# Norm statistics by sums on ScalarE, and attention weights of four steps added by accumulating DMAs

## The chip, the cores and the metric

The kernel runs on one core of a Trainium2 chip. The metric is the device time of one execution in microseconds (us). A run is one execution; medians are over several runs of the same kernel.

Engines, as the profile names them: PE is TensorE's matmuls, PEld its weight loads, DVE VectorE, ACT ScalarE, POOL GpSimd, SP SyncE. SPq and POOLq are the queues on which SP and GpSimd issue DMAs.

## The reference, cut to what matters

Sixteen graphs ("batches") of 1024 nodes with 256 features go through four layers. Each layer normalises its input; three are graph attention, the fourth is a small transformer block of eight heads of 32 features.

```python
def _layernorm(x, axis=-1, eps=1e-5):
    m = jnp.mean(x, axis=axis, keepdims=True)
    v = jnp.var(x, axis=axis, keepdims=True)
    return (x - m) / jnp.sqrt(v + eps)
...
# layers 0 to 2: h = relu(layernorm(x)); x = x + graph_attention(h, adj, W, a)
# layer 3, on h = relu(layernorm(x)), with H = 8 heads of D = 32:
scores = jnp.einsum('fnhd,fmhd->fhnm', q, k) / sqrt(D)
scores = jnp.where(mask, scores, -1e9)
attn = softmax(scores, axis=-1)
t = jnp.einsum('fhnm,fmhd->fnhd', attn, v).reshape(F, N, C)
x = _layernorm(x + t, ln1_g, ln1_b)
h = relu(x @ w1 + b1)
x = _layernorm(x + h @ w2 + b2, ln2_g, ln2_b)
```

Two things matter here: the means and variances of the norms, and the denominators of layer 3's softmax, which are sums of the exponentials over all 1024 keys.

## The kernel before

The kernel contains its own planner. Every operation is recorded with an engine, an estimated duration and the buffers that it reads and writes; `schedule` then plays the engines against each other and fixes the order of each engine at build time. Priorities come from a few numbers, the "constants" (`GATS`, `VALUES`, `STEPS`, `FEED`, `LEAD`, `BIAS`).

Layer 3 walks through `steps` of (group of four heads `g`, half of the rows `hf`, block of 128 keys `jt`). A step makes the scores of four heads, takes the exponential on ScalarE and multiplies by the mask on VectorE, into two tiles `pa` of 128 x 1024 fp32 (512 KB each). A "quad" of matmuls on 32 columns each then multiplies them with the values, and another quad with a tile of ones gives the denominators. In three of the four groups of a batch, the weights of two steps were first added on VectorE, so that one ones quad served two steps:

```python
                if paired(g, hf) and jt % 2:
                    sums[n] = [r_sums.new() for _ in range(2)]
                    for ss, p0, p1 in zip(sums[n], pas[n - 1], pas[n]):
                        dve(tt_us(2 * HALF), lambda: nc.vector.tensor_add(ss.t, p0.t, p1.t), [ss], [p0, p1])
```

The projections for the scores are split into a high and a low part and copied into stacks `qs` and `ks` by 16 small DMAs from SP. `hi` and `lo` are single buffers, and a projection shares its four PSUM buffers `sc` with the scores.

```python
            pe(CT * mm_us(HALF), product, [sc], ...)          # sc: one of 4 PSUM buffers
            act(act_us(HALF), lambda: nc.scalar.copy(hi.t.bitcast(F32R), sc.t), [hi], [sc])
            dve(tt_us(HALF), lambda: nc.vector.tensor_sub(lo.t, sc.t, hi.t), [lo], [sc, hi])
            for a in range(4):
                part = ((hi, hi, lo, lo), (hi, lo, hi, lo))[keys][a]
                for r in range(HG):
                    dma(0.33, lambda: nc.sync.dma_start(
                            stack.t[a * D3 : (a + 1) * D3, r, at : at + HALF],
                            part.t[r * D3 : (r + 1) * D3, :]), ..., us=0.635)
        ...
        later = {
            (0, 0, 2): [(queries, 0, 1)],
            (0, 1, 2): [(queries, 1, 0)],     # issued during group (0, 1)
            (0, 1, 4): [(keys, 1, 0)],
            (1, 0, 0): [(keys, 1, 1)],
            (1, 0, 2): [(queries, 1, 1)],
        }
```

Norm statistics were made on VectorE, 256 features at a time:

```python
    def stats(src, src_ref, dst, dst_ref, whose="g"):
        st = r_st[whose].new()
        dve(0.342, lambda: nc.vector.bn_stats(st.t, src), [st], [src_ref])
        dve(0.11, lambda: nc.vector.bn_aggr(dst, st.t), [dst_ref], [st])
```

Of the kernel before, what the change touches and what calls it, by code (L numbers as in the profile page):

```python
# [16 lines left out]
AF = mybir.ActivationFunctionType  # L17
# [242 lines left out]
LANDING = 2.5  # L260
BIAS = 0.648
LEAD = {"act": -0.527, "dve": 0.112}
# [38 lines left out]
def direct(ctx, tc, flag, x, adj, gat_w, gat_a, w_qkv, ln1_g, ln1_b, ln2_g, ln2_b, w1, b1, w2, b2, out):  # L301
# [12 lines left out]
        (-0.447, -0.367, -0.162, 0.113, 0.24),  # L314
        (0.384, 0.522, 0.626, 0.731, 0.828),
        (0.805, 0.841, 0.856, 0.879, 1.02),
    )
    VALUES = (1.045, 1.057, 1.088, 1.245, 1.191)
    STEPS = (1.289, 1.484, 1.664, 1.807, 1.951)
    FEED = (2.178, 2.28, 2.353, 2.529, 2.38)  # L320
# [37 lines left out]
    r_st = {k: ring(f"st{k}", 4, [6]) for k in "gf"}  # L358
    r_hn = ring("hn", 1, [TH, C])
# [46 lines left out]
    def dve(us, emit, w, r):  # L406
        rec.add("dve", us, emit, w, r)
# [7 lines left out]
    def stats(src, src_ref, dst, dst_ref, whose="g"):  # L415
        st = r_st[whose].new()
        dve(0.342, lambda: nc.vector.bn_stats(st.t, src), [st], [src_ref])  # L417
        dve(0.11, lambda: nc.vector.bn_aggr(dst, st.t), [dst_ref], [st])

# [213 lines left out]
    def gat(xt, b_mv, b_rstd, l):  # L633
# [8 lines left out]
        for hf in range(2):  # L642
# [3 lines left out]
            inverse(mv[:, l, s, 0], mv[:, l, s, 1], rstd[:, l, s], mv_refs, rstd_ref)  # L646
# [142 lines left out]
        for hf in range(2):  # L789
            s = slice(hf * TH, (hf + 1) * TH)  # L790
            if H == 1:
                row = spread(hf, 0, rds[hf])
                pts = [weights(hf, 0, jt, row) for jt in range(NT)]
                for k in range(TH):
# [55 lines left out]
                    dve(tt_us(C), lambda: nc.vector.tensor_add(xs, xs, ex), [xt(it)], [b_ex(0)])  # L850
                    if l != 1:
                        dve(
                            tt_us(C),
                            lambda: nc.vector.tensor_sub(xs, xs, eo),
                            [xt(it)],
                            [b_ex(1)],
                        )
                    stats(xs, xt(it), mv[:, l + 1, it, :], b_mv((l + 1, it)))
# [116 lines left out]
    def attention(b, xt, b_mv, b_rstd):  # L975
# [3 lines left out]
        for hf in range(2):  # L979
# [3 lines left out]
            inverse(mv[:, 3, s, 0], mv[:, 3, s, 1], rstd[:, 3, s], mv_refs, rstd_ref)  # L983
# [122 lines left out]
        def quad(ac, jt, of_head, columns, first, last):  # L1106
            for r in range(HG):
                nc.tensor.matmul(  # L1108
                    ac.t[r * D3 : (r + 1) * D3, :],
                    columns(r),  # L1110
                    of_head(r),
                    start=first,
                    stop=last,
                )

        def value(n, both):

            g, hf, jt = steps[n]
            for ac in accs[g, hf][: 1 + both]:
                quad(  # L1120
                    ac,
                    jt,
                    lambda r: pas[n][r // 2].t[:, r % 2, :],
                    lambda r: (
                        ones
                        if ac is accs[g, hf][1]
                        else va.t[:, jt, (g * HG + r) * D3 : (g * HG + r + 1) * D3]
                    ),
                    jt == 0,
                    jt == NT - 1,  # L1130
                )

        def paired(g, hf):

            return g == 1 or hf == 1
# [4 lines left out]
        for n in range(len(steps) + LAG):  # L1140
            m = n - LAG
            if m >= 0:
                g, hf, jt = steps[m]
                if jt == 0:
                    accs[g, hf] = [r_bank.new(), r_bank.new()]
                both = not paired(g, hf)
                pe(
                    (1 + both) * 0.855,
                    lambda: value(m, both),
                    accs[g, hf],  # L1150
# [3 lines left out]
                if not both and jt % 2:  # L1154
                    ss = sums[m]
                    pe(
                        0.855,
                        lambda: quad(
                            accs[g, hf][1],
                            jt,  # L1160
                            lambda r: ss[r // 2].t[:, r % 2, :],
                            lambda r: ones,
                            jt == 1,
                            jt == NT - 1,
                        ),
                        [accs[g, hf][1]],
                        ss,
                        ("col4", "col4"),
                    )
# [51 lines left out]
            if n < len(steps):  # L1221
# [56 lines left out]
                if paired(g, hf) and jt % 2:  # L1278
                    sums[n] = [r_sums.new() for _ in range(2)]
                    for ss, p0, p1 in zip(sums[n], pas[n - 1], pas[n]):  # L1280
                        dve(
                            tt_us(2 * HALF),
                            lambda: nc.vector.tensor_add(ss.t, p0.t, p1.t),  # L1283
                            [ss],
                            [p0, p1],
                        )
# [3 lines left out]
    def feed(b, x3, hn):  # L1290
# [95 lines left out]
        def back(hf):  # L1386
            yT = yTs[hf]
            for it in (hf * TH, hf * TH + 2):
# [32 lines left out]
                act(act_us(HALF), lambda: nc.scalar.copy(z_t, pz()), [z(0), z(1)], [g])  # L1421
                for k in range(2):
                    stats(z_t[:, k, :], z(k), mvz.t[:, k, :], mvz(k), "f")
                inverse(
                    mvz.t[:, :, 0], mvz.t[:, :, 1], rstdz.t, [mvz(0), mvz(1)], rstdz, False
                )
                for k in range(2):
# [8 lines left out]
                            op0=ALU.subtract,  # L1436
# [29 lines left out]
    def batch(b):  # L1466
# [12 lines left out]
        for it in range(NT):  # L1479
            stats(xt.at(it), xt(it), b_mv.t[:, 0, it, :], b_mv((0, it)))  # L1480
# [630 lines left out]
```

## Time and profile before

| kernel before | |
|---|---|
| time | 4209.74 us, median of 3 runs (4208.88 to 4213.89) |
| PE, DVE, ACT, POOL busy | 98, 88, 55, 10% of the span |
| TensorE idle | 33 us in the first 200, 20 in the last 109, 18.5 from 200 to 3800 |

The page's chain of work that ended last, as shares of the span by engine:

```profile
PE 80%; DVE 12%; DMA 2%; SPq 2%; issue 2%; POOL 1%; ACT 1%; DVEq 0%; ACTq 0%
```

Two rows of waits (engine, tile and line that waited, what ended the wait, us in total, times, longest):

```profile
DVE pt L774 <- DMA row<-rd: 78.6, 30, 7.3
...
ACT pa L1259 <- DVE sums L1283: 54.8, 28, 2.7
```

### The profile page before, as it was taken

Reading aid. Unit: us, or ns where it says so; the run is one execution under the profiler, and the core shown is the slowest. Engines: PE = TensorE matmul, PEld = TensorE weight load, DVE = VectorE, ACT = ScalarE, POOL = GpSimd, SP = SyncE. Lnnn points to the kernel's source line nnn. Section 1 sums busy time; section 2 is a strip of 40 time slices with the busy share of each in tenths; the row PEclk is TensorE's granted clock in tenths of the full one; section 3 lists DMA queues with packets and bytes.
Section 4 is the critical chain, followed back from the end, with each engine's and each line's share of the span. In section 5 each row is a group of like instructions: output and inputs, shape, how many; then the busy total and the mean of one; then the engine's idle time right before and its main releaser. Section 6 shows DMA issues by size and latency. Waiting matters only on the chain.

```text
span 4208.8 us, 68595 instructions
## 1 busy us (share of the span) xinstructions
PE 4133.7 (98%) x24738; PEld 2399.0 (57%) x24738; DVE 3710.0 (88%) x6786; ACT 2333.7 (55%) x5041; POOL 427.2 (10%) x391
## 2 busy tenths in 40 slices
PE   7999999999999999999999999999999999999998
PEld 3746556564665646556465564646656465564643
DVE  7589898998989889898998979989898898989977
ACT  3445555564655746556555555646556465565564
POOL 0001001011010101001010010110111010010110
PEclk9999999999999999999999999999999999999998
DMA  3121222212222122221212222122221222212131
GB/s 104 48 64 42 81 61 66 66 36 81 58 74 61 51 65 57 76 71 52 66 45 81 61 66 66 36 81 59 73 60 50 65 58 76 69 49 67 44 86 36
DMA packets 180683, 263.82 MB, mean 63 GB/s; under 512 B 41328, under 2 KB 76400, under 8 KB 180336
## 3 DMA queue, kind: packets, MB, share of 16 engines
q1 hardware_dynamic: 180336, 259.36, 22.5%
q8 instruction: 198, 3.24, 0.3%
q14 instruction: 149, 1.22, 0.1%
HBM read 91.03 MB, written 33.95 MB: 30 GB/s over the span
## 4 chain that ended last, share of the span: by engine, by line
PE 80%; DVE 12%; DMA 2%; SPq 2%; issue 2%; POOL 1%; ACT 1%; DVEq 0%; ACTq 0%
PE bank L801 21%; PE bank L1108 16%; PE sc L1235 10%; PE bank L677 8%; DVE pt L774 7%; PE bank L875 6%; PE bank L474 5%; PE sc L1024 5%; PE bank L1341 4%; PE bank L885 3%; DVE pa L1268 2%; PE sc L1060 2%; SPq L1045 2%; DMA row<-rd 1%; POOL rstdz L426 1%
## 5 line engine op out<-in xcount | busy, mean ns | idle before, releaser
L1259 ACT ACTIVATE pa<-sc 128x512 f32<-128x512 f32 x2048 | 1096.4, 607 | 588.4 <-PE sc L1235 448.6
L1268 DVE TENSOR_TENSOR pa<-pa,mask 128x1024 f32<-128x1024 f32 x1024 | 1210.1, 1211 | 12.4 <-ACT pa L1259 12.0
L774 DVE SCALAR_TENSOR_TENSOR pt<-row,e,mask 128x512 f32<-128x512 f32 x1536 | 1058.5, 740 | 107.5 <-DMA row<-rd 78.6
L801 PE MATMUL bank<-qb,pt 128*128 128x257 f32 x4096 | 942.8, 381 | 0.5 <-ACT ex L829 0.4
L801 PEld LDWEIGHTS bank<-qb,pt 128*128 128x128 f32 x4096 | 770.6, 190 | 166.5 <-issue 21.8
L1235 PE MATMUL sc<-qs,ks 128*128 128x512 f32 x2048 | 700.4, 448 | 1.9 <-ACT pa L1259 1.3
L1108 PE MATMUL bank<-pa,va 128*32 128x512 f32 x4096 | 543.5, 597 | 7.4 <-DVE pa L1268 7.0
L875 PE MATMUL bank<-pt,qb 128*32 128x512 f32 x4096 | 511.5, 596 | 4.7 <-DVE pt L774 4.7
L1235 PEld LDWEIGHTS sc<-qs,ks 128*128 128x128 f32 x2048 | 358.0, 188 | 223.7 <-ACT pa L1259 102.7
L1283 DVE TENSOR_TENSOR sums<-pa,pa 128x1024 f32<-128x1024 f32 x384 | 454.6, 1213 | 7.0 <-PE bank L1108 6.5
L677 PE MATMUL bank<-w_aug,hT 128*128 128x259 f32 (+1 forms) x1536 | 372.8, 391 | 0.6 <-ACT mask L587 0.2
L426 POOL TENSOR_TENSOR rstd<-rstd,neg_half 128x4 f32<-128x4 f32 x160 | 200.7, 1257 | 1499.8 <-DVE rstd L423 1340.9
L677 PEld LDWEIGHTS bank<-w_aug,hT 128*128 128x128 f32 x1536 | 289.4, 192 | 94.4 <-issue 15.3
L875 PEld LDWEIGHTS bank<-pt,qb 128*32 128x32 f32 x4096 | 132.8, 109 | 303.4 <-issue 210.3
L829 ACT ACTIVATE ex<-bank,rec 128x256 f32<-128x256 f32 x256 | 121.6, 476 | 324.0 <-DVE rec L821 321.1
L885 PE MATMUL bank<-pt,e 128*32 128x512 f32 x2048 | 288.4, 593 | 0.0
L1108 PEld LDWEIGHTS bank<-pa,va 128*32 128x32 f32 x4096 | 118.8, 109 | 283.1 <-issue 196.5
L445 ACT ACTIVATE hn<-xt,mv,rstd 128x256 f32<-128x256 f32 x384 | 204.2, 598 | 87.7 <-DVE mv L435 87.7
L906 ACT COPY ot<-bank 128x512 f32<-128x512 f32 x128 | 75.0, 586 | 318.7 <-PE bank L875 269.7
L1024 PE MATMUL sc<-hTa,wqkv_sb 128*128 128x512 f32 x512 | 239.9, 595 | 1.0 <-ACT hTa L1009 0.5
L1108 PE MATMUL bank<-sums,ones 128*32 128x512 f32 x1536 | 216.4, 597 | 0.7
L417 DVE BATCH_NORM_STATS2 stg<-xt 128x6 f32<-128x256 f32 x512 | 208.9, 414 | 3.2
(107 smaller groups left out, 4053.0 us busy)
## 6 DMA issues: line engine op xcount, KB each, us to landing
row<-rd SPq DMA_DIRECT2D x192, 256.0 KB
ks<-hi SPq DMA_DIRECT2D x512, 64.0 KB
ks<-lo SPq DMA_DIRECT2D x512, 64.0 KB
qs<-hi SPq DMA_DIRECT2D x512, 64.0 KB
qs<-lo SPq DMA_DIRECT2D x512, 64.0 KB
xt<-in_x_dram SPq DMA_DIRECT2D x32, 512.0 KB
x<-xt SPq DMA_DIRECT2D x32, 512.0 KB
xr<-x SPq DMA_DIRECT2D x64, 256.0 KB
```

What stands on the lines that cost most here:

```text
L426: lambda: nc.gpsimd.tensor_tensor(out=rstd, in0=rstd, in1=neg_half[:, :n], op=ALU.pow),
L677: nc.tensor.matmul(g.t[:, : C + 3 * H], hT.t[:, ct, k * P : (k + 1) * P], w_aug[l][:, ct, :], start=ct == 0, stop=ct == CT - 1,)
L774: lambda: nc.vector.scalar_tensor_tensor(pt.t, row.t, e3[:, 2, jt // TH, h, jt % TH : jt % TH + 1], mask[:, jt, hf * HALF : (hf + 1) * HAL ...
L801: nc.tensor.matmul(g.t[:, : D + 1], pts[jt].t[:, k * P : (k + 1) * P], qb[:, jt, 0, :], start=jt == 0, stop=jt == NT - 1,)
L875: nc.tensor.matmul(g.t[u * D + d : u * D + d + D3, :], qb[:, j, h + u, d : d + D3], pts[u][j - jt].t, start=j == 0, stop=j == NT - 1,)
L885: nc.tensor.matmul(gd.t[c : c + D3, :], one(jt + k, h + u).to_broadcast([P, D3]), pts[u][k].t, start=jt == 0, stop=jt == NT - 2,)
L1024: nc.tensor.matmul(sc.t, wqkv_sb[:, ct, c0 : c0 + P], hT.t[:, ct, hf * HALF : (hf + 1) * HALF], start=ct == 0, stop=ct == CT - 1,)
L1108: nc.tensor.matmul(ac.t[r * D3 : (r + 1) * D3, :], columns(r), of_head(r), start=first, stop=last,)
L1235: nc.tensor.matmul(scs[r - r0].t, ks.t[:, r, jt * P : (jt + 1) * P].bitcast(F32R), q.t[:, r, :].bitcast(F32R), start=True, stop=True,)
L1259: lambda: nc.scalar.activation(pt.t[:, v, :], sc.t, AF.Exp, scale=1.0 / math.sqrt(D3)),
L1268: lambda: nc.vector.tensor_mul(pt.t, pt.t, mask[:, jt : jt + 1, i0 : i0 + HALF].to_broadcast([P, 2, HALF]),),
L1283: lambda: nc.vector.tensor_add(ss.t, p0.t, p1.t),
```

## The change

The intent is to take work from TensorE (fewer ones quads) and from VectorE (statistics), and to give it to ScalarE and to the DMA engines, which have room. Means come as a by-product of the last add on VectorE or of a copy on ScalarE, and variances as a sum of squares on ScalarE. The weights of four steps are added in the groups with `hf == 1`, the third and the fourth step by a DMA that adds to its target; the other groups add two steps; the last batch adds none.

```diff
-LANDING = 2.5
-BIAS = 0.648
-LEAD = {"act": -0.527, "dve": 0.112}
+LANDING = 2.8
+BIAS = 0.939
+LEAD = {"act": 2.715, "dve": 0.501}
 ... (GATS, VALUES, STEPS, FEED: other numbers too)
+    def spread_of(srcs, src_refs, sums, squares, refs):
+        act(0.19, lambda: nc.scalar.mul(sums, sums, -1.0 / C), refs, [])
+        for k, (src, src_ref, ref) in enumerate(zip(srcs, src_refs, refs)):
+            act(act_us(C, 1) + 60e-3,
+                lambda: nc.scalar.activation(waste.t, src, AF.Square,
+                    bias=sums[:, k : k + 1], accum_out=squares[:, k : k + 1]), [ref], [src_ref])
 ... (the end of a graph layer)
-                    dve(tt_us(C), lambda: nc.vector.tensor_add(xs, xs, ex), [xt(it)], [b_ex(0)])
-                    ...
-                    stats(xs, xt(it), mv[:, l + 1, it, :], b_mv((l + 1, it)))
+                    dve(stt_us(C) + 60e-3,
+                        lambda: nc.vector.scalar_tensor_tensor(
+                            xs, xs, 0.0, last, op0=ALU.add, op1=op, accum_out=total), ...)
 ... (layer 3)
-        def paired(g, hf):
-            return g == 1 or hf == 1
+        def run_of(g, hf):
+            return 1 if b == NB - 1 else 4 if hf == 1 else 2
 ...
+                run = run_of(g, hf)
+                if jt % run == 1:
+                    sums[g, hf] = [r_sums.new() for _ in range(2)]
+                    ... (ss = p0 + p1 on VectorE, as before)
+                elif jt % run:
+                    for ss, pt in zip(sums[g, hf], pas[m]):
+                        dma(3.0, lambda: nc.gpsimd.dma_start(ss.t, pt.t, accum_op=ALU.add),
+                            [ss], [pt], us=0.88, engine="pool")
 ... (the value quad)
+                if jt % run == run - 1:
+                    ss = pas[m] if run == 1 else sums[g, hf]
+                    ... (one ones quad for the run)
```

The second norm of the feed-forward and the first norm of each batch change in the same way; the statistics of the first feed-forward norm and those of one graph layer stay as they were.

## The prediction

> **What bounds the kernel now.** I read the busy table first, then the same numbers by stretches of time, then the order of TensorE's matmuls, and the groups that the change touches last.
>
> ```profile
> PE 4133.7 (98%) x24738; PEld 2399.0 (57%) x24738; DVE 3710.0 (88%) x6786; ACT 2333.7 (55%) x5041; POOL 427.2 (10%) x391
> ...
> PE   7999999999999999999999999999999999999998
> ```
>
> TensorE is at 98%, VectorE at 88%, ScalarE at 55%, GpSimd at 10%. A busy TensorE need not be a full one, so I asked where it is not busy, by stretches (columns: stretch, its length, then busy time and instructions of PE, PEld, DVE, ACT, POOL, then clock, DMA share, GB/s):
>
> ```profile
> 0.00:100.00 100.00, 76.94 (x528) 34.08 (x530) 81.10 (x176) 28.62 (x57) 4.48 (x12) 0.95 0.32 109
> 100.00:200.00 100.00, 89.96 (x392) 70.84 (x387) 53.28 (x153) 43.44 (x108) 9.52 (x14) 0.93 0.11 36
> ...
> 2000.00:2600.00 600.00, 595.99 (x3722) 335.02 (x3712) 542.80 (x986) 332.99 (x715) 61.25 (x54) 1.00 0.22 62
> ...
> 4100.00:4209.00 109.00, 89.28 (x386) 33.65 (x384) 85.00 (x134) 50.78 (x94) 5.60 (x7) 0.90 0.14 36
> ```
>
> Of the 75 us in which TensorE is idle (4208.8 - 4133.7), 33 lie in the first 200 us and 20 in the last 109. In the middle it is idle for 4 us of 600. There VectorE with 543 of 600 is not what TensorE waits for; the program fixes the order ahead of time, and other batches fill the gaps. So in the middle the time is the sum of what TensorE is given, and work taken from VectorE alone buys next to nothing.
>
> The timeline of TensorE's matmuls (start, duration, line, tiles, count) says what one unit of that work is worth. Durations overlap, so I go by start to start:
>
> ```profile
> 1016.50 1.92 PE L875 MATMUL bank<-pt,qb 128*32 128x512 f32 x16
> 1018.24 1.04 PE L885 MATMUL bank<-pt,e 128*32 128x512 f32 x8
> 1019.10 1.90 PE L875 MATMUL bank<-pt,qb 128*32 128x512 f32 x16
> 1020.81 1.04 PE L885 MATMUL bank<-pt,e 128*32 128x512 f32 x8
> 1021.79 1.20 PE L1235 MATMUL sc<-qs,ks 128*128 128x512 f32 x4
> 1022.91 1.92 PE L875 MATMUL bank<-pt,qb 128*32 128x512 f32 x16
> ```
>
> Eight records on 32 columns each (four fp32 matmuls of two passes, a "quad" below) take 0.86 us in a stream (1018.24 to 1019.10). Four score matmuls between other 128-column work take 0.92 us (0.23 each, from the trace's starts). From 1016.50 to 1022.91 there are six quads and four scores, 6 x 0.858 + 0.92 = 6.07, but 6.41 passed: leaving the 32-column work and coming back to it costs 0.34 us. Over the whole trace the return trips without an evident wait give a median of 0.34 to 0.36 us. I count 352 such blocks in the kernel before.
>
> **What the Trainium skill says.** "Perfetto Trace Analysis", section "Identifying the Most-Contended Engine": matmul busy time is not a good measure of distance from the roofline, because matmuls are pipelined. I agree for this trace, where the quad's records read 1.04 us for a step of 0.86, and therefore use steps. "TensorEngine Tiling (Array Packing)", section "Key Properties": changing the tiling mode drains TensorE; the 0.34 us above is this trace's number for it. "DMA: Bandwidth & Descriptors", section "Anatomy of one DMA": a DMA issued by GpSimd takes about 2.0 us plus bytes / 436e3; a section further on (SWDGE vs HWDGE vs iDMA) says that accumulating needs this path. The kernel before has none, so no run here shows it yet. "ScalarE: Activation LUTs", section "What ACT_TABLE_LOAD costs": 186 ns + 0.833 per element with immediates, 93 more per pointer operand, so 399 and 492 ns for 256 elements; the trace has 425 (the second Relu of the ELU) and 476 (the scaled Relu), within 7%. For the accumulator output the page has no price.
>
> **The change, part by part.** The groups that it touches:
>
> ```profile
> L1283 DVE TENSOR_TENSOR sums<-pa,pa 128x1024 f32<-128x1024 f32 x384 | 454.6, 1213 | 7.0 <-PE bank L1108 6.5
> ...
> L1108 PE MATMUL bank<-sums,ones 128*32 128x512 f32 x1536 | 216.4, 597 | 0.7
> L417 DVE BATCH_NORM_STATS2 stg<-xt 128x6 f32<-128x256 f32 x512 | 208.9, 414 | 3.2
> ...
> L1108 PE MATMUL bank<-pa,ones 128*32 128x512 f32 x1024 | 149.5, 593 | 0.0
> ```
>
> *Denominators on TensorE.* Before, each batch spends 8 quads with the ones in its first group and 4 in each of the other three: 20, times 16 batches = 320 (the counts agree: (1536 + 1024) / 8). After, batches 0 to 14 spend 4 + 2 + 4 + 2 = 12, and the last batch sums nothing and spends 32: 180 + 32 = 212. So 108 quads go, at 0.858 us = -92.7 us. But the order of the built kernel has 430 32-column blocks instead of 352: the sums' quads now often stand between scores instead of next to a value quad. 78 x 0.34 = +26.5 us. Net on the bounding engine: **-66 us**.
>
> *Sums on VectorE.* 24 adds per batch stay (16 for the pairs of two groups, 8 for the first pairs of the runs of four), and 24 of the last batch go: -24 x 1.18 = -28 us.
>
> *Statistics on VectorE.* 384 of the 512 statistics of xt and the 128 of the second norm of the feed-forward go, each with its aggregation: 512 x about 0.56 (busy time by group) = -287 us. In return 256 plain adds become adds with a total, some 0.06 to 0.12 dearer: +15 to +30. With the sums VectorE falls from 3710 to about 3420 us. By the stretches above this is off the path except at the ends.
>
> *ScalarE.* Per batch 16 copies with a total (0.43), less 4 wide copies (0.62), 32 squares with a pointer (0.48) and 10 small scalings (0.2): about 22 us, or +345 us, to some 2680 us, 65%. Off the path, but the way through a norm gets longer: four squares can only follow all four totals, about 2 us later than an aggregation did.
>
> *DMA and GpSimd.* 15 batches x 2 groups x 2 runs x 2 steps x 2 tiles = 240 transfers of 512 KB. By the skill's formula, an estimate, 2.0 + 1.2 = 3.2 us each; reading the target as well makes it nearer 4.5. They run two and two, and the fourth step's must wait until the third's have landed. In the order of the built kernel, the work that lies on TensorE between the last score of a run of four and the quad that reads its sum is at least 13.2 us (by the steps above), in the median 16. What must fit: an exponential 0.6, a mask product 1.2, two issues of perhaps 1 us each, two transfers of 2.5 us one behind the other and a landing of 2, some 11 us. So mostly hidden, with little room in about 15 of the 60 cases.
>
> *The ends.* The last batch runs without a next one beside it. There VectorE has 2.4 + 1.2 us per step (two mask products, and one add on average) against about 2.6 of TensorE. Without sums it has 2.4 and TensorE 3.1; of 20 us idle I expect some 10 to 15 to go (the 12 quads more are counted above). The first 200 us are a single batch's chain, and the longer norms may cost about 5 there.
>
> Sum: 4210 - 66 - 12 + 5 = 4137. VectorE's lower load should take away some of the short waits of the middle (20 us idle, and by the steps some 57 us above the plain sum), and I give it 10 us, less a few for late sums: **4130 us**.
>
> **The rivals.** *Late sums.* If an accumulating transfer takes 6 us instead of 3 to 4, or the descriptors take GpSimd several us, TensorE, whose order is fixed, stands at some of the 60 sums quads for 2 to 6 us, and 1/sqrt of the norms stands behind the transfers in GpSimd's queue: +60 to +200 us, so 4190 to 4330. For it: no such transfer in the trace; against: 13 to 16 us of cover. *Contention of transfers.* The DMA share is 22% now, and 240 x 512 KB add at least 126 MB to 259. The rows' broadcasts already make VectorE wait (78.6 us in 30 waits) and could be held up by a few us each: +10 to +40 us. *VectorE was the hidden bound*, through buffers that it frees late: then taking 8% of its work gives more than the sum, 4080 to 4100. Against it are the 4 us of 600. *Switching dearer than counted*, with most of the gain lost in the drains: 4150 to 4170.
>
> **Range and chances.** The quads (-93) are certain, the switches are uncertain by 10, the bubbles by 25 and the sums by more on the slow side. 8 in 10: 4095 to 4172. Faster by over 2% means under about 4127, which is almost the middle: 0.44. Within 2%: 0.52. Slower by over 2%: 0.04.
>
> **What would show it.** TensorE still at 98 to 99% and its records down by 864 to 23874; 848 ones matmuls in program terms (1696 records); VectorE near 3420, ScalarE near 2680. Sums in time: waits of TensorE on a landing of the accumulating transfer below 15 us in all. Wrong if those waits exceed 60 us, if GpSimd's 1/sqrt is late and the norms stop TensorE, or if TensorE's idle time in the middle stretches falls or rises by more than 10 us in 600.

## More of the kernel before

A transfer is planned like this, with a queue for each issuing engine of its own:

```python
            if x.moved:
                queue[e] = max(at + 0.2, queue[e]) + x.moved
                x.pass_on = queue[e] + LANDING - (at + us)
```

VectorE carries 12% of the chain though TensorE is hardly ever idle: the chain goes through VectorE at times. Its longest wait for a transfer is for the rows that are broadcast for the graph attention.

## The result, and the profile after

| | median of 4 runs | range |
|---|---|---|
| before | 4211.11 us | 4208.88 to 4213.89 |
| after | 4155.49 us | 4152.05 to 4163.23 |
| ratio | 0.9870 | 0.9853 to 0.9887 (95%) |

A ratio is the mean time of one kernel's fast runs over that of the other's of the same rounds, so it is not quite the ratio of the medians quoted. The change is worth 1.3%: within 2%, inside the range, and 25 us above the predicted 4130.

The busy table of the kernel after, and from the same page its chain by engine, its two large DMA queues (packets, MB, share of 16 engines' span) and the row of its accumulating transfers (count, KB each, median us from issue to landing):

```profile
PE 4049.7 (98%) x23874; PEld 2358.5 (57%) x23874; DVE 3504.5 (84%) x5994; ACT 2680.9 (65%) x6673; POOL 558.7 (13%) x631
...
q1 hardware_dynamic: 180336, 259.36, 22.3%
q0 software_dynamic: 34560, 125.84, 16.0%
...
PE 79%; ACT 8%; DVE 6%; DMA 2%; SPq 2%; issue 2%; POOL 0%; DVEq 0%; ACTq 0%
...
sums<-pa POOLq DMA_DIRECT2D x240, 512.0 KB, 5.9
```

TensorE is busy as large a share as before. Half of VectorE's share of the chain has gone, and ScalarE has taken as much. A queue that did not exist before uses 16.0% of the DMA engines: 0.160 x 4150.3 / 240 = 2.8 us of all sixteen for each transfer.

The stretches of the kernel after (columns as in the prediction):

```profile
0.00:100.00 100.00, 77.92 (x535) 34.77 (x536) 78.46 (x162) 42.22 (x110) 6.14 (x13) 0.97 0.32 109
100.00:200.00 100.00, 88.81 (x386) 72.12 (x384) 42.48 (x119) 52.02 (x153) 6.89 (x12) 0.90 0.09 29
...
2000.00:2600.00 600.00, 592.54 (x3548) 344.29 (x3541) 531.23 (x900) 393.90 (x986) 85.93 (x93) 1.00 0.40 96
...
4050.00:4151.00 101.00, 83.21 (x487) 34.16 (x486) 65.25 (x102) 58.57 (x132) 5.80 (x7) 0.95 0.17 44
```

The ends have hardly moved: 33.3 us of TensorE idle in the first 200 (33.1 before), 17.8 in the last 101 (19.7 in the last 109 before). The middle has become worse: 7.5 us idle of 600 where it was 4.0, and 40.7 from 200 to 3800 where it was 18.5.

The groups that the change touched, by form (columns as in the prediction):

```profile
L1188 DVE TENSOR_TENSOR sums<-pa,pa 128x1024 f32<-128x1024 f32 x360 | 435.6, 1221 | 30.3 <-PE bank L1161 25.3
...
L1161 PE MATMUL bank<-sums,ones 128*32 128x512 f32 x1440 | 193.5, 599 | 0.2 <-DMA sums<-pa 0.2
...
L418 DVE BATCH_NORM_STATS2 stg<-xt 128x6 f32<-128x256 f32 x128 | 49.3, 416 | 0.0
...
L1161 PE MATMUL bank<-pa,ones 128*32 128x512 f32 x256 | 37.6, 593 | 0.0
```

The ones quads fell from 2560 records to 1696, as counted. They idle 0.2 us for a landing of the sums, so the sums are in time.

**The time taken apart.** Busy time hides short stands between matmuls, so I took TensorE's matmul records of each trace and worked with their starts. Each kind of matmul has a median step from its start to the next start (for example 0.2175 us for the 257 columns of the graph layers, 0.4293 for 512 columns, 0.230 for scores, 0.1073 for a record of a quad). Count times step is the *plain sum*. Blocks of 32-column work times 0.345 us are the *switches*. What is left between the first and the last matmul's start is the *rest*: all waiting and all slowness. I give the rest of the stretch from 250 to 3890 us apart.

| us | plain sum | switches (blocks) | rest | of it 250 to 3890 |
|---|---|---|---|---|
| before | 3920 | 121 (352) | 144 | 54 |
| after | 3827 | 148 (430) | 153 | 80 |
| difference | -93 | +27 | +9 | +26 |

The three differences make -57, and the profiled spans differ by -58.5 (4208.8 and 4150.3). So the two certain terms of the prediction came out as worked, and the rest, which should have shrunk by some 14 us (ends -7, middle -10 and a few for late sums), grew by 9.

Where does the middle lose? The waits have two rows which answer to those of before, and two new ones:

```profile
ACT pa L1319 <- DVE sums L1188: 68.3, 36, 5.0
...
DVE pt L813 <- DMA row<-rd: 35.8, 24, 7.3
PE sc L1295 <- DVE lo L1089: 35.7, 14, 4.2
...
PEld bank L1161 <- DMA sums<-pa: 2.8, 4, 1.1
```

TensorE stood 14 times before scores, 2.5 us on average, until VectorE had made a low part `lo`. Before, PE had no such wait for the scores of attention steps (line 1235 of that kernel). Fourteen is close to one for each of the fifteen batches that add by DMA. The rows' broadcasts, which I had feared for, wait less than before, and the sums quads wait for landings for 2.8 us in the whole kernel.

One of the fourteen, in stretches of 5 us around it (columns as before: the last three are clock, DMA share and GB/s), and then its timeline (start, duration, engine and line, operation, tiles; in brackets the idle time before it and what ended that):

```profile
2825.00:2830.00 5.00, 5.00 (x24) 4.03 (x22) 5.00 (x9) 2.54 (x5) 0.40 (x1) 1.00 0.57 110
2830.00:2835.00 5.00, 5.00 (x31) 1.91 (x31) 4.43 (x7) 2.59 (x6) 1.38 (x2) 1.00 1.04 234
2835.00:2840.00 5.00, 2.19 (x10) 1.53 (x9) 1.54 (x5) 2.01 (x4) 1.56 (x2) 1.00 1.06 218
2840.00:2845.00 5.00, 4.93 (x15) 3.97 (x16) 4.59 (x8) 2.25 (x5) 0.17 (x1) 0.66 0.99 211
```

```profile
2827.88 7.89 SPq L1098 DMA_DIRECT2D qs<-lo  x8
...
2829.60 0.92 POOL L1196 DMA_DIRECT2D sums<-pa  x1 [9.63 <-DVE sums L1188]
...
2832.77 1.98 PE L1077 MATMUL sc<-hTa,wqkv_sb 128*128 128x512 f32 x4
...
2835.87 4.89 SPq L1098 DMA_DIRECT2D ks<-hi  x4
...
2836.61 0.58 PE L1295 MATMUL sc<-qs,ks 128*128 128x512 f32 x1
...
2839.32 0.69 DVE L1089 TENSOR_TENSOR lo<-sc,hi 128x512 f32<-128x512 f32 x1 [3.46 <-DMA qs<-lo]
...
2840.07 1.43 PE L1295 MATMUL sc<-qs,ks 128*128 128x512 f32 x3 [2.87 <-DVE lo L1089]
```

Read it from the top. SP issues the eight copies of the low part of the queries of group (1, 0), which takes 7.89 us. Among them GpSimd issues accumulating transfers, and the DMA engines are full: a share of 1.04, then 1.06, at 234 and 218 GB/s (the share adds up the times of packets, which must overlap where it passes 1). Meanwhile TensorE has made the projection of the keys (2832.77). Its low part must go into the one buffer `lo`, which the copies of the queries still read, so VectorE, whose order is fixed, stands 3.46 us. The projection's PSUM buffer is one of the four that the scores use, and the scores stand 2.87 us until VectorE has read it.

The stand costs more than its own length. In the last of the four stretches the granted clock is 0.66: its record reads 0.5 from 2840.3 to 2843.8 us, and there the matmuls of 257 columns go at steps of 0.43 us in place of 0.2175. Between 250 and 3890 us this trace has eight stretches at 0.5, of 3.4 or 6.8 us, and each begins 2.8 to 4.5 us after the last matmul start before one of these stands. The eight stands were 2.9 to 4.7 us long; two others of 3.5 and 3.8 us and all shorter ones were not followed by such a stretch. By steps, the matmuls in the eight stretches lost some 16 us. The kernel before has no such stretch there, and no two of its matmul starts there lie more than 1.3 us apart.

### The profile page after: what moved, and what is told of

Read it like the earlier page. It is cut to its first block, busy times and chain, and to the rows that moved or that the text cites. A ratio compares the mean times of both kernels' runs of the same rounds, so it can differ in the third digit from the quotient of the medians.

```text
span 4150.3 us, 68028 instructions
## 1 busy us (share of the span) xinstructions
PE 4049.7 (98%) x23874; PEld 2358.5 (57%) x23874; DVE 3504.5 (84%) x5994; ACT 2680.9 (65%) x6673; POOL 558.7 (13%) x631
## 3 DMA queue, kind: packets, MB, share of 16 engines
q1 hardware_dynamic: 180336, 259.36, 22.3%
q0 software_dynamic: 34560, 125.84, 16.0%
## 4 chain that ended last, share of the span: by engine, by line
PE 79%; ACT 8%; DVE 6%; DMA 2%; SPq 2%; issue 2%; POOL 0%; DVEq 0%; ACTq 0%
PE bank L840 18%; PE bank L1161 12%; PE sc L1295 10%; PE bank L927 10%; PE bank L716 7%; PE bank L512 5%; PE bank L937 5%; PE bank L1392 5%; PE sc L1077 4%; ACT waste L429 2%; PE sc L1113 2%; SPq L1098 2%; DVE pa L1328 2%; ACT pa L1319 1%; DVE pt L813 1%
## 5 line engine op out<-in xcount | busy, mean ns | idle before, releaser
L1319 ACT ACTIVATE pa<-sc 128x512 f32<-128x512 f32 x2048 | 1108.1, 607 | 448.7 <-PE sc L1295 317.5
L813 DVE SCALAR_TENSOR_TENSOR pt<-row,e,mask 128x512 f32<-128x512 f32 x1536 | 1068.1, 747 | 49.6 <-DMA row<-rd 35.8
L1161 PE MATMUL bank<-pa,va 128*32 128x512 f32 x4096 | 514.7, 597 | 1.3 <-DVE pa L1328 1.0
L1188 DVE TENSOR_TENSOR sums<-pa,pa 128x1024 f32<-128x1024 f32 x360 | 435.6, 1221 | 30.3 <-PE bank L1161 25.3
L716 PE MATMUL bank<-w_aug,hT 128*128 128x259 f32 (+1 forms) x1536 | 391.2, 393 | 2.1 <-ACT hT L710 1.9
L1196 POOL DMA_DIRECT2D sums<-pa x240 | 210.5, 877 | 1059.4 <-DVE rec L860 239.0
L927 PEld LDWEIGHTS bank<-pt,qb 128*32 128x32 f32 x4096 | 122.3, 109 | 296.5 <-issue 224.0
L429 ACT ACTIVATE waste<-xt,mv 128x256 f32<-128x256 f32 x384 | 196.2, 511 | 7.0
L1161 PE MATMUL bank<-sums,ones 128*32 128x512 f32 x1440 | 193.5, 599 | 0.2 <-DMA sums<-pa 0.2
L1086 ACT CAST hi<-sc 128x512 fp32r<-128x512 f32 x128 | 74.5, 582 | 178.9 <-PE sc L1077 76.9
```

The costliest lines, as they stand in the source:

```text
L429: lambda: nc.scalar.activation(waste.t, src, AF.Square, bias=sums[:, k : k + 1], accum_out=squares[:, k : k + 1]),
L716: nc.tensor.matmul(g.t[:, : C + 3 * H], hT.t[:, ct, k * P : (k + 1) * P], w_aug[l][:, ct, :], start=ct == 0, stop=ct == CT - 1,)
L813: lambda: nc.vector.scalar_tensor_tensor(pt.t, row.t, e3[:, 2, jt // TH, h, jt % TH : jt % TH + 1], mask[:, jt, hf * HALF : (hf + 1) * HAL ...
L927: nc.tensor.matmul(g.t[u * D + d : u * D + d + D3, :], qb[:, j, h + u, d : d + D3], pts[u][j - jt].t, start=j == 0, stop=j == NT - 1,)
L1161: nc.tensor.matmul(ac.t[r * D3 : (r + 1) * D3, :], columns(r), of_head(r), start=first, stop=last,)
L1319: lambda: nc.scalar.activation(pt.t[:, v, :], sc.t, AF.Exp, scale=1.0 / math.sqrt(D3)),
```

## The experiments

Four theories for the missing 25 us, the first two of which are rivals for the same stands:

- **Contention.** The bytes of the accumulating transfers fill the DMA engines just when SP's stack copies need them. The cure is fewer bytes at that moment.
- **The order.** The new order itself puts the copies and the scores too close, or the many small issues do; the transfers' bytes don't matter.
- **VectorE matters.** I had called its load off the path. If it is on it after all, the statistics gave more than counted and hid a larger loss.
- **Late sums**, which the 2.8 us above already speak against.

All expectations below are from before the runs. Where they number the theories, 1 is contention and 2 the order; their theory 3 is that GpSimd's queue, with the transfers in it, makes the 1/sqrt of the norms late. Where only the accumulating line is replaced, the planner sees the same record as before, so each engine keeps its order.

| kernel | median us | ratio to before (95%) | gaps over 1 us within scores: number, us | rest | of it 250 to 3890 |
|---|---|---|---|---|---|
| after | 4155.5 | 0.9870 (0.9853 to 0.9887) | 15, 45.2 | 153 | 80 |
| none_added (wrong) | 4101.1 | 0.9743 (0.9726 to 0.9759) | 1, 1.3 | 99 | 28 |
| half_bytes (wrong) | 4107.3 | 0.9755 (0.9739 to 0.9771) | 7, 10.4 | 108 | 36 |
| two_halves | 4155.9 | 0.9866 (0.9850 to 0.9883) | 14, 38.1 | 156 | 82 |
| gpsimd_adds | 4524.6 | 1.0749 (1.0731 to 1.0767) | 30, 119.6 | 525 | 393 |
| one_by_dve | 4152.8 | 0.9862 (0.9846 to 0.9879) | 6, 10.5 | 150 | 76 |
| both_by_dve | 4271.0 | 1.0141 (1.0124 to 1.0158) | 16, 41.3 | 273 | 182 |
| stats_alone | 4243.1 | 1.0080 (1.0063 to 1.0097) | 2, 2.6 | 138 | 39 |
| stats_alone_replanned | 4179.4 | 0.9927 (0.9912 to 0.9943) | 2, 3.0 | 91 | 3 |
| sums_alone_old | 4419.6 | 1.0487 (1.0470 to 1.0505) | 2, 6.4 | 426 | 342 |
| sums_alone_replanned | 4264.3 | 1.0126 (1.0111 to 1.0142) | 14, 52.2 | 264 | 182 |
| one_queue | 4136.7 | 0.9827 (0.9812 to 0.9842) | 2, 3.5 | 129 | 51 |
| one_queue_q_early | 4131.1 | 0.9815 (0.9801 to 0.9828) | 0, 0 | 126 | 54 |

The kernel before has no such gap. The plain sum is 3920 for the two kernels with the statistics alone and 3827 for the others but before. All results were correct except for the two that are wrong on purpose. Matmuls at half clock are part of the rest: between 250 and 3890 us they lost some 16 us in after, 11 in two_halves, 88 in gpsimd_adds, 34 in both_by_dve, 43 in sums_alone_old and 23 in sums_alone_replanned. The other kernels, the kernel before among them, have no half-clock stretch there.

### Without the transfers

```diff
-                            lambda: nc.gpsimd.dma_start(ss.t, pt.t, accum_op=ALU.add),
+                            lambda: None,
```

The third and fourth steps are missing from the sums, so the result is wrong (relative error 0.07).

> The 240 accumulating transfers are left out, everything else keeps its place in every engine's order (the result is wrong on purpose: the third and fourth step are missing in the sums). Theory 1 (the transfers hold the DMA engines while the copies of q and k into their stacks run, so the first scores of a group come late once per batch, 49 us in all by the start times of the matmuls): the once-per-batch gap of 2.9 to 4.7 us at the scores goes below 1 us and the time is 4105 to 4120 us. Theory 2 (the fixed order puts that projection of q too late, whatever the transfers do): the gap stays at 3 to 4 us and the time at 4145 to 4160. Theory 3 (GpSimd's queue makes the 1/sqrt late): the gap at the scores stays, other idle time of TensorE in the middle falls, 4130 to 4150.

Measured: 4101.13 us, 54 less than after. The gaps within scores go from 15 (45.2 us) to 1 (1.3 us), and the rest of the middle from 80 to 28. Of these 52 us, 39 are steps of over 1 us between matmul starts (less the matmuls' own) and 16 the half clock; other terms give 3 back. The same copies in SP's queue in this trace:

```profile
2798.84 4.94 SPq L1098 DMA_DIRECT2D qs<-lo  x8
...
2806.02 2.41 SPq L1098 DMA_DIRECT2D ks<-hi  x4
```

They take 4.94 and 2.41 us where they took 7.89 and 4.89, in the same order of instructions. Over the whole trace, 14 of 48 such groups of eight took more than 6 us with the transfers, and 1 of 48 without. So the transfers cost 54 us, which makes the order theory fall for them, and without them the middle is better than before the change (28 against 54). What this run can't tell is whether it is their bytes, their number or GpSimd's issue of them.

### Half of each transfer

```diff
-                            lambda: nc.gpsimd.dma_start(ss.t, pt.t, accum_op=ALU.add),
+                            lambda: nc.gpsimd.dma_start(ss.t[:, 0, :], pt.t[:, 0, :], accum_op=ALU.add),
```

Wrong as well: the same 240 transfers, of 256 KB each.

> Same order, same 240 accumulating transfers, but each moves half of its columns (wrong result on purpose). Theory 1: the gap at the scores shrinks to about 1 to 2.5 us, time 4120 to 4140, between no transfers and whole ones. Theory 2: as the changed kernel, 4145 to 4160. Theory 3: as the changed kernel too, since GpSimd issues as many transfers.

Measured: 4107.34 us, below the expected 4120 to 4140, so 48 of the 54 us go with half of the bytes. The number of issues is the same, and GpSimd is as busy (562.0 us against 558.7). The landing falls from 5.9 to 3.6 us in the median, SP's eight copies take 5.69 us, and the stands before scores nearly vanish; in the waits:

```profile
PE sc L1295 <- DVE lo L1089: 5.8, 7, 1.2
```

Neither the number of transfers nor their issue matters then, but the bytes do, and far from in proportion: half of them cost 6 us, all of them 54. The half clock is one reason that the traces show: with half of the bytes no two matmul starts in the middle lie more than 1.9 us apart and no stretch at half clock follows. That the DMA engines are full at that moment or not would be another; it is argued and not shown apart.

### The same bytes in twice as many transfers

```diff
-                            lambda: nc.gpsimd.dma_start(ss.t, pt.t, accum_op=ALU.add),
+                            lambda: [nc.gpsimd.dma_start(ss.t[:, a, :], pt.t[:, a, :], accum_op=ALU.add) for a in range(2)],
```

> The changed kernel's order and bytes, but each accumulating transfer of 512 KB (pieces of 4 KB a partition) is issued as two of 256 KB with pieces of 2 KB (result correct). Half the bytes brought the time from 4155 to 4107 us; that run also halved the pieces. If the bytes count (the engines are simply full while q is copied): the gap at the scores stays at 3 us or more and the time is 4145 to 4170. If the size of the pieces counts (a small copy waits behind each long piece): the gap falls under 2 us and the time is 4105 to 4125.

Measured: 4155.9 us, the same as after (4155.5). The wait is there again:

```profile
PE sc L1295 <- DVE lo L1089: 29.6, 14, 4.8
```

Smaller pieces let SP's copies in no earlier: eight of the low part in the same batch took 8.04 us. GpSimd's 240 more issues (777.6 us busy in place of 558.7) cost nothing, so its queue (theory 3) isn't the cause either.

### One of the two tiles added by VectorE

```diff
-                    for ss, pt in zip(sums[g, hf], pas[m]):
-                        dma(3.0, lambda: nc.gpsimd.dma_start(ss.t, pt.t, accum_op=ALU.add), ...)
+                    for u, (ss, pt) in enumerate(zip(sums[g, hf], pas[m])):
+                        def join():
+                            if u:
+                                nc.vector.tensor_add(ss.t, ss.t, pt.t)
+                            else:
+                                nc.gpsimd.dma_start(ss.t, pt.t, accum_op=ALU.add)
+                        dma(3.0, join, [ss], [pt], us=0.88, engine="pool")
```

> The changed kernel's order, but of the two tiles of a step VectorE adds one and a transfer the other (result correct): 120 transfers instead of 240, and 120 adds of 1.22 us more on VectorE, at the place in its queue where the transfer stood. Theory 1 (transfers fill the DMA engines): the gap at the scores under 2 us; VectorE has the room for 146 us (3504 to 3650, 89%); time 4105 to 4130, under both kernels. Rival: VectorE's adds come in the way of mask products and TensorE waits for them instead: 4140 to 4180.

Measured: 4152.76 us, as the rival had it. It moves the same bytes as half_bytes (62.92 and 62.93 MB), and the gaps within scores agree (6 of 10.5 us, 7 of 10.4). But it is 45 us slower than half_bytes. The transfers differ only in number (120 whole ones, 240 halves), which two_halves shows to cost nothing; what is left are 120 adds on VectorE, 145.9 us of work. What grew, from 39.6 us in 58 waits in half_bytes, is the wait of the scores' weight loads for the exponentials:

```profile
PEld sc L1294 <- ACT pa L1318: 71.5, 130, 1.6
```

A third of what VectorE was given turned up in the time. "Off the path" was wrong: VectorE isn't the bound, but in an order that is fixed its delays reach TensorE through buffers. The planner didn't know of these adds, so this is their price in an order made without them.

### Both tiles added by VectorE

```diff
-                            lambda: nc.gpsimd.dma_start(ss.t, pt.t, accum_op=ALU.add),
+                            lambda: nc.vector.tensor_add(ss.t, ss.t, pt.t),
```

> As one_by_dve, with both tiles added by VectorE: no transfers at all, 240 adds of 1.22 us more on VectorE (3504 to 3797, 92%; result correct). Theory 1: the gap at the scores is gone, as without any adds (4101 us), but VectorE's own work now comes late in places: 4110 to 4150. If VectorE truly is off the path, 4101 to 4110. If VectorE's room was used up: over 4160.

Measured: 4270.99 us, 170 more than none_added, which has neither adds nor transfers. VectorE is busy 3758.6 us, 257 more than there. The exponentials now hold up the matmuls too, where in none_added it was 3.5 us in 7 waits:

```profile
PE sc L1295 <- ACT pa L1319: 35.2, 22, 2.3
```

All 240 adds cost 170 us, some 34 of them through the half clock, where the 240 transfers cost 54. So in this order, which was planned for transfers, they were the better way to add, though not a free one.

### Both tiles added by GpSimd

```diff
-                            lambda: nc.gpsimd.dma_start(ss.t, pt.t, accum_op=ALU.add),
+                            lambda: nc.gpsimd.tensor_tensor(out=ss.t, in0=ss.t, in1=pt.t, op=ALU.add),
```

> Same order, but the third and fourth step are added by a GpSimd instruction in the transfer's place instead of by the transfer (result correct). Theory 1: the gap at the scores goes below 1 us; if an add of 128x1024 takes GpSimd under 4 us, the time is 4105 to 4130. Theory 2: the gap stays, 4145 to 4160. Theory 3, and the risk in this experiment itself: GpSimd is busier (240 adds of perhaps 2 to 3 us), norms come later, and VectorE may be slowed as both read two operands; then 4140 to 4200.

Measured: 4524.57 us, the slowest of all and far above all that was expected. The groups of GpSimd's adds, and the durations of the mask products on VectorE (count, then ns as minimum, median and maximum):

```profile
L1196 POOL TENSOR_TENSOR sums<-sums,pa 128x1024 f32<-128x1024 f32 x240 | 688.6, 2880 | 944.2 <-DVE pa L1328 334.4 <-DVE rec L860 250.2 <-DVE sums L1188 214.9
```

```profile
L1328 DVE TENSOR_TENSOR pa<-pa,mask x1024: 1155/1220/3417, 232.9 to 4484.6; 128x1024 f32<-128x1024 f32 x171
```

An add takes 2.88 us, and some mask products take up to 3.42 us in place of 1.22. VectorE is busy 3960.8 us, 459 more than in none_added, without one instruction more. The Trainium skill's page "SBUF — State Buffer", section "Who interferes with whom", says that VectorE's second pair of ports is shared with GpSimd and is an exclusive lock. This trace agrees with it: operations on two tiles get longer where GpSimd's adds run. Against the median of the same operation in none_added, those that overlap an add took 472 us more in all, the others 0.1 us. The page also says that DMA has ports of its own, separate from the engines'. With the accumulating DMAs VectorE is as busy as without them (3504.5 and 3501.5 us), so this trace agrees there too.

### The statistics alone

```diff
-            return 1 if b == NB - 1 else 4 if hf == 1 else 2
+            return 1 if (g, hf) == (0, 0) else 2
```

This is the kernel after with the sums of the kernel before, and the constants of after.

> The changed kernel with the sums as before (first group of each batch unsummed, pairs in the other three, also in the last batch): norm statistics alone, under the changed kernel's constants of order. 320 quads with the ones as before, 457 blocks of 32-column work instead of 352, so by steps +36 us on TensorE. If VectorE is off the path, as the prediction has it: 4225 to 4255. If VectorE was a hidden bound and the statistics are where the gain comes from: under 4190.

Measured: 4243.13 us, slower than before by 0.8%, and inside the range for a VectorE that is off the path. But it has 457 blocks of 32 columns, 105 more than before: 158 us of switches against 121. The constants of after place another kernel's work. The rest of its middle is 39 (54 before). So this run said less than I had hoped, and it was done again with constants of its own. I searched them with nothing but the forecast of the kernel's own planner, and ran the best:

```diff
-BIAS = 0.939
-LEAD = {"act": 2.715, "dve": 0.501}
+BIAS = 0.854
+LEAD = {'act': 1.306, 'dve': -0.523}
 ... (the other constants too)
```

> Norm statistics alone (sums as before), its order's constants searched again, since stats_alone ran under constants found for other work: 422 blocks instead of 457. If VectorE is off the path: by steps 4211 + (422 - 352) x 0.34 = 4235 less what shorter waits give, 4190 to 4235. If the statistics are the gain by themselves: under 4170.

Measured: 4179.37 us, 31 less than before and between the two expected ranges, with 422 blocks and a rest of 3 us in the middle. VectorE has gone from 3710.0 to 3525.8 us. So it is likely, but not shown, that statistics which leave VectorE pay by themselves on a kernel whose TensorE was 98% busy. How much of the 31 us a search for the unchanged kernel would have found as well is open; between the two sets of constants lie 64 us for this one kernel.

### The sums alone

First the kernel before with the new sums and its own old constants:

```diff
-        def paired(g, hf):
-            return g == 1 or hf == 1
+        def run_of(g, hf):
+            return 1 if b == NB - 1 else 4 if hf == 1 else 2
 ... (the whole hunk of layer 3; nothing else of the change)
```

> The kernel before with the new sums alone (runs of four with transfers, none in the last batch), norm statistics and the constants of the order as before. 212 quads and 421 blocks instead of 320 and 352: by steps -93 + 24 = -69 us on TensorE, plus what the transfers cost here (0 to 60 us) and VectorE at 88%. If the gain is TensorE's quads: 4140 to 4190. If the statistics' relief of VectorE is needed for it: over 4200.

Measured: 4419.62 us. The order is bad, as the waits of the weight loads for exponentials show:

```profile
PEld sc L1242 <- ACT pa L1266: 204.6, 300, 4.4
```

Then the same with constants of its own, searched with a planner that has one queue for all transfers (the edit is shown further on):

```diff
-LANDING = 2.5
-BIAS = 0.648
+LANDING = 2.28
+BIAS = 0.911
 ... (the other constants too)
```

> The sums alone (statistics on VectorE as before), planned with one queue and constants searched again: 438 blocks, 212 quads. If sums_alone_old was slow (4420) through its order and the transfers' contention: 4150 to 4210, that is better than before. If VectorE, with the statistics on it, has no room for the sums' later release of the weights' buffers: over 4250 still.

Measured: 4264.31 us, 54 more than before, though the plain sum is 93 lower. The 14 stands within scores are here as well (52.2 us), and the exponentials wait for tiles `pa` which the adds have not yet read (54.8 us before):

```profile
ACT pa L1266 <- DVE sums L1135: 273.1, 108, 6.8
```

So the statistics alone give -31, the sums alone +54, and together they give -55. The two parts depend on each other: taken alone, with the constants that were found for them, the sums lose. I read it as follows, argued and not shown apart: a run of four holds its tiles longer, VectorE must then read them in time, and it can do so only once the statistics are off it.

### One queue in the planner, and the queries earlier

Last, two versions that should beat both kernels if contention is the cause. In the first the planner knows that SP's and GpSimd's transfers share the DMA engines; the constants were searched again with it (BIAS 0.819 and others).

```diff
-                queue[e] = max(at + 0.2, queue[e]) + x.moved
-                x.pass_on = queue[e] + LANDING - (at + us)
+                queue["dma"] = max(at + 0.2, queue["dma"]) + x.moved
+                x.pass_on = queue["dma"] + LANDING - (at + us)
```

> As one_queue_q_early without the earlier projection: only the planning with one queue and the constants searched again. Theory 1: 4105 to 4135, part of the way, as the q copies still have little room. Transfers dear by themselves: 4140 or more.

Measured: 4136.73 us, 19 less than after and just over the expected 4105 to 4135. The gaps within scores are down to 2 (3.5 us), and the rest of the middle is 51; with 448 blocks it pays 6 us more for switches.

In the second the projection of the queries of group (1, 0) is also made two steps earlier, before the group's first accumulating transfer, again with constants of its own.

```diff
-            (0, 1, 2): [(queries, 1, 0)],
+            (0, 1, 0): [(queries, 1, 0)],
```

> The changed kernel with the same instructions, but its order planned anew: the planner in the kernel's own text counts the accumulating transfers and all others in one queue (it kept one for each issuing engine), the projection of q for the third group is put two steps earlier in the program, and the order's constants are searched again under this planner. If contention with the copies of q and k, not foreseen by the plan, was what kept the changed kernel from its gain (theory 1): the gap at the scores is gone with all 240 whole transfers in place, and the time is 4095 to 4120 us, faster than both. If the transfers cost by themselves, whenever they run: 4140 or more.

Measured, in 5 rounds: 4131.10 us (4130.21 to 4134.09), a ratio of 0.9815. It beats the kernel after by 24 us and the kernel before by 79, with the same 240 transfers and 125.84 MB, and no gap over 1 us within scores. It is the fastest correct kernel here. The expected range, 4095 to 4120, was missed all the same. The rest of its middle is still 54 against the 28 of none_added. What these 26 us are is open; a row that grew is this one, 40.4 us in none_added:

```profile
PEld sc L1295 <- ACT pa L1319: 71.1, 122, 0.9
```

A second `lo` buffer would be another cure for the same stand. It was not tried.

## Why the prediction was right or wrong

The time was inside the range and the most likely of the three outcomes came true. None of the prediction's signs of being wrong appeared: the sums quads waited 2.8 us for landings (the sign was 60), and TensorE's idle time in the middle rose by 2 to 5.4 us of 600 (the sign was 10). Two of its steps were wrong nevertheless; the signs were too coarse to show it. By its steps:

1. **Ones quads and switches, -93 and +26.5: right.** The steps of the trace give -93 and +27, and a return trip to 32-column work has a median of 0.344 us in the kernel after. Taking durations from start to start, and counting blocks in the built order and not in the diff, made this term hold.
2. **ScalarE at 2680 us: right** (2680.9), in part by luck. The terms left out the separate reads of its accumulator, 153 us summed over their groups; counting overlaps of neighbours once took about as much away. **VectorE at about 3420: 84 too low** (3504.5). I had subtracted busy times of groups. These fell, summed over all groups, by 255 us (I had some 285 to 300), of which the totals' separate reads of the accumulator, 256 times 85 ns, are 22. And the page's busy time fell only by 205, because neighbours overlap in the groups and are counted once in the page.
3. **"By the stretches above this is off the path except at the ends": the step that failed.** At a fixed order 146 us of VectorE work cost 45 us, 257 us cost 170; the statistics alone, replanned, gave 31, an unknown part of it by the new search. What I read as proof, 4 us of TensorE idle in 600, only says that TensorE is rarely idle in the profile, and not that its steps are undisturbed: the rest, which contains the short stands, was 54 us in the middle. I gave this term "10 us, less a few"; measured without the transfers the middle gains 26 (54 to 28). The trace of before has it, by steps: in its middle 27 steps are over 1 us, 31 us in all, and each was ended by VectorE (13 by `ex`, 14 by a mask product). none_added has 3. As its order is planned anew too, how much of the 26 is VectorE's lower load isn't shown.
4. **Transfers "mostly hidden": the other half that failed.** I had asked only whether the sums land in time, and they do: the median landing was 5.9 us and not my 4.5, and the sums quads still waited only 2.8 us in all. That rival fell as I had argued. But the transfers cost 52 us in the middle (28 to 80) at another place, some 16 of them as matmuls at half clock after the stands, which no part of the prediction had. "Contention of transfers" was the right rival, with 10 to 40 us a little too small and the wrong victim: the rows' broadcasts wait less than before (35.8 us against 78.6) and no less without the transfers (36.8), while the stack copies hold the single buffer `lo` for longer and so VectorE, a PSUM buffer and the scores, about once a batch. The Trainium skill would have told me where to look: "DMA: Bandwidth & Descriptors", section "Issuing engines are not separate DMA queues", says that transfers from any engine run on the same 16 DMA engines and interleave. The prediction didn't use it and treated GpSimd's transfers as if they ran beside SP's; this trace agrees with the page (SP's eight copies took 7.89 us of issue in place of 4.94), and the kernel's planner, with a queue for each issuer, had made the same mistake.
5. **The ends, -12 + 5: small either way.** By idle time they gained 2 us (the first 200 unchanged, the last 101 down from 19.7 to 17.8). By the steps the rest outside 250 to 3890 fell by 17 (90 to 73). The two ways bracket the -7.

So of the predicted -80 some -57 came (-66 for the first step in both; -14 predicted for everything else, +9 measured). The error is the sum of two larger ones of opposite sign in points 3 and 4: 26 us gained where I had 10 and 52 lost where I had a few. The kernel that keeps the transfers from the copies runs at 4131, which is what I had predicted for a kernel whose transfers are hidden; but as its order is another, that agreement proves nothing about the single terms.

## What to carry to other kernels

Before you add traffic to DMA engines with a low mean share, look at the moments when other transfers that hold a single buffer are due, in stretches of a few microseconds: 39% on average (22.3 + 16.0 + 0.4 in the page's queues) was 104% there. Look at the granted clock after a stand as well: of the ten stands of 2.9 us or more in the middle of the kernel after, eight were followed by matmuls at half clock. If a planner fixes the order at build time, let all issuing engines share one queue in its model, and search its constants again for every variant that you compare, or "one part alone" measures the constants. An engine that is never the bound may still set when buffers come free; price its load by adding to it on the chip, and not by the idle time of the busiest engine.

## What the Trainium skill lacked or had wrong

- "DMA: Bandwidth & Descriptors", section "Anatomy of one DMA — SWDGE (gpsimd) path": its fit gives 3.2 us for 512 KB. The accumulating transfers took 4.5, 5.9 and 8.2 us (minimum, median, maximum), and 4.4, 4.8 and 7.9 us when there were half as many. For 256 KB it gives 2.6, and 3.6 was measured. No section prices accumulation: here it took 2.8 us of all sixteen engines for 512 KB, or 0.160 x 4150.3 / 125.84 = 5.3 us for each MB, against 0.223 x 4150.3 / 259.36 = 3.6 for the kernel's other transfers.
- The same page, section "Issuing engines are not separate DMA queues", is right, and calls the time to initiate a DMA usually small relative to the DMA. It doesn't say that traffic slows it: while the engines were full, SP took 7.89 us to issue eight copies of 64 KB (32 partitions of 512 fp32), and 4.94 us for the same eight without the accumulating transfers.
- "TensorEngine Tiling (Array Packing)", section "Key Properties", names the drain at a change of tiling without a price: 0.34 us for leaving 32-column work and coming back.
- "ScalarE: Activation LUTs" has no price for the accumulator's output. It is a record of its own here, 191 ns after each square of 256 elements, which itself takes 511 ns with one pointer operand.
- "SBUF — State Buffer", section "Who interferes with whom", has the rule, and ratios for single operations, but no price for a whole kernel: beside 240 GpSimd adds of 2.88 us each, VectorE's busy time rose by 459 us and the kernel's time by 423 us (4101 to 4525).
